# Rows of a rank block in 120 neighbouring partitions instead of two halves of 60, and the fetch of the blocks in four transfers instead of eight

## The chip, the core and the metric

The kernel runs on one core of one Trainium2 chip. Time is device time in microseconds (us), from the first to the last thing that the program does on that core. Several runs are timed and their median is given; one more execution is recorded by the hardware profiler, and all views of the profile come from that execution.

## The reference

For each of 32 batches x is a matrix of 512 channels by 1024 nodes, and adj is 512 by 512. Two layers follow each other, each with a residual sum and a layer norm over the 1024 nodes:

```python
# layer 0
q = einsum('c,bcn->bn', wq, x)
k = einsum('c,bcn->bn', wk, x)
scores = leaky_relu(q[:, None, :] + k[:, :, None], 0.01)   # m by n
att = softmax(scores, axis=-1)
agg = einsum('bcn,bmn->bcm', x, att)
x = layernorm(x + relu(einsum('oc,bcm->bom', adj, agg) + bm[None, :, None]))
# layer 1
x = layernorm(x + (einsum('bnf,nm->bmf', x, adj * adj) + bias))
```

The score of a pair (m, n) is q[n] + k[m]. Where the sum is positive its exponential is exp(q[n]) times exp(k[m]); where it is negative it is exp(0.01 q[n]) times exp(0.01 k[m]). So if the nodes n are sorted by q, what node m needs is one sum over the nodes with the largest q, weighted by exp(q), and one over the rest, weighted by exp(0.01 q). The kernel never forms the 1024 by 1024 attention matrix: it makes tables of these running sums, and each node m picks its rows from them.

## The kernel before

All numbers of lines are those of the profile.

**Tiles and stages of one batch.** `project` (L329) multiplies x by the transposed adj and by wq and wk on TensorE (PE). `keep` brings the result into `zrow`: 1024 rows of 514 numbers, q, then 512 projected values, then a 1. `place` (VectorE, L394) counts for every node its rank by q. `send` (GpSimd, L406) scatters the rows of `zrow` by rank into a buffer `td` in DRAM; `td` has for every rank three rows side by side: the row itself and two places for table rows. `fetch` (L445 to L460) brings the rows back in the order of rank into `zs`. `weigh_exp` (L467, ScalarE) makes the weights `w`, `weigh_by` (L479, L487, VectorE) makes from them and the triangular masks `tri` the small matrices `lw` that sum within a block. `table` (L501, PE) multiplies, `table_out` (L513, ScalarE) copies the product out of PSUM, `carry` (L519) puts the running total into the next block, `table_store` (L527, SyncE's queue, SP) writes table rows to `td`. `pick` (L534, GpSimd) gathers for every node m its own row and two table rows, `scale` and `gain` (L573, L578) mix them, `turn` (L587) transposes, `add` (L594) adds x. The second layer is `multiply` (L666) and the two layer norms are around it.

**Blocks.** The 1024 ranks are cut into nine blocks of R = 120 (the last holds 64). A block is one column of `zs`: its ranks lie in the partitions, in two halves of RH = 60. Half 0 lies in partitions 1 to 60, half 1 in 65 to 124. Partition 0 holds the running total that the sum from the top (i = 0) brings from the block above, partition 64 that of the sum from the bottom (i = 1). The rest are fillers of weight zero. One table row is made for every second rank, so a block gives 60 rows of each table.

**Steps.** `blocks(step)` names the two blocks of a step: 8 - step for the sum from the top and step for the sum from the bottom. `t0` to `t8` are the nine steps of `table`; both products of a step go to one PSUM tile, rows 0 to 63 and 64 to 127. `e0` to `e8` are `table_out`. After each step but the last, `cp` (carry i = 0, on GpSimd) copies row 0 of the result into partition 0 of block 7 - step, and `ca` (carry i = 1, on ScalarE) copies row 64 into partition 64 of block step + 1. At step 3 both go to block 4. The next step waits for its two carries.

**The fetch.** `fetch` issues eight transfers on SP: the last block in two pieces (60 rows and 4), then blocks 0 and 1, block 7, and blocks 2 to 6, each of these once for half 0 and once for half 1. Part 0 of the weights (`wx0`, `wb0`) needs all but blocks 2 to 6, and `t0` needs `wb0`. Part 1 (`wx1`, `wb1`) needs blocks 2 to 6 and is needed at `t2`.

**The order of the work** is written out by hand: the strings BEGIN, SLOT and END list the steps, and each engine runs its instructions in that order. SLOT is the steady state. It works on four batches at once: in one pass the ranks of batch s + 2 are made and sent, the tables of s + 1 and the second layer of s are made, and the output of s - 1 is stored. `fe` (fetch) is SLOT's last step; `wx0 wb0 t0` of the same batch come early in the next pass. Around step 3 the plan reads:

```python
    # SLOT: ... t3 k1u2 k1p5 gb5 p24 gb4 e3 ca3 u0 ts3 cp3 av2 so3 t4 ad0 ...
    # END:  ... @31 e2 ca2 cp2 t3 e3 ca3 cp3 @29 av0 ro1 @31 t4 ...
```

Waits between engines follow from what overlaps: a copy that writes a partition which another copy has written before it in this order waits for that one. SP has eight semaphores for its transfers in turn, so a transfer also waits until the eighth before it has landed.

Of the kernel before, what the change touches and what calls it, by code (L numbers as in the profile page):

```python
# [13 lines left out]
ALU = mybir.AluOpType  # L14
# [9 lines left out]
def gat_gcn_resnorm_kernel(  # L24
# [11 lines left out]
    nc = tc.nc  # L36
    P = 128
    B, C, N = x.shape
# [5 lines left out]
    ZW = C + 2  # L44
    ZB = ZW + 1
    SC = 32.0
    G = P // 2
    RH = 60
    R = 2 * RH
    NB = N // R + 1  # L50
    LAST = N - (NB - 1) * R
# [23 lines left out]
    for i, a in enumerate((wq, wk, bm)):  # L75
        nc.scalar.dma_start(
            out=vec[i * CT : (i + 1) * CT, :], in_=a.rearrange("(t p) -> t p", p=P)
# [6 lines left out]

    tri = const.tile([P, 2, G], F32, name="tri")
    nc.vector.memset(tri, 1.0)
    for half in range(2):
        p0 = half * G
        nc.gpsimd.affine_select(
            out=tri[p0 : p0 + G, 0, :], in_=tri[p0 : p0 + G, 0, :], pattern=[[-2, G]],  # L90
            compare_op=ALU.is_ge, fill=0.0, base=half * RH, channel_multiplier=1,
        )
        nc.gpsimd.affine_select(
            out=tri[p0 : p0 + G, 1, :], in_=tri[p0 : p0 + G, 1, :], pattern=[[2, G]],
            compare_op=ALU.is_ge, fill=0.0, base=-2 - half * RH, channel_multiplier=-1,
        )
    nc.vector.memset(tri[:, :, 0:1], 1.0)
    for row, i in ((0, 0), (G, 1)):
        nc.vector.memset(tri[row : row + 1, i, :], 1.0)
        nc.vector.memset(tri[row : row + 1, 1 - i, :], 0.0)  # L100

    el = const.tile([P, 2], F32, name="el")
    nc.vector.memset(el[:, 0:1], 1.0)
    nc.vector.memset(el[:, 1:2], NEG_SLOPE)
    nc.vector.memset(el[0:1, :], 0.0)
    nc.vector.memset(el[G : G + 1, :], 0.0)
    nel = const.tile([P, 2], F32, name="nel")
    nc.vector.tensor_scalar(nel, el, -1.0, None, ALU.mult)

# [3 lines left out]
        out=first, in_=first, pattern=[[-1, 2 * N - P]], compare_op=ALU.is_ge,  # L113
        fill=0.0, base=N - P - 1, channel_multiplier=1,
# [3 lines left out]
    zs = const.tile([P, NB, ZB], F32, name="zs")  # L118
    nc.vector.memset(zs, 0.0)
    nc.vector.memset(zs[:, :, 0:1], FAR)  # L120
    nc.vector.memset(zs[:, :, C + 1 : ZW], 1.0)
    for row in (0, G):
        nc.vector.memset(zs[row : row + 1, :, C + 1 : ZW], 0.0)

    xs, vs = {}, {}
    for b in range(B):
# [15 lines left out]
    for td in tdb:  # L142
        nc.sync.dma_start(
            out=td.rearrange("(s u) c -> s u c", u=3)[N:NS, 0, :], in_=zs[P + N - NS : P, 0, 0:ZW]
        )
        odd = td.rearrange("(s w u) c -> s w (u c)", w=2, u=3)
        for r in range(0, NS // 2, P):
            n = min(P, NS // 2 - r)
            nc.sync.dma_start(
                out=odd[r : r + n, 0, ZW : 3 * ZW].rearrange("p (j c) -> p j c", j=2)[:, :, 0:1],  # L150
                in_=zs[0:n, 0:2, 1:2],
            )
            nc.sync.dma_start(
                out=odd[r : r + n, 1, ZW : 3 * ZW].rearrange("p (j c) -> p j c", j=2),
                in_=zs[0:n, 0:2, 0:ZW],
# [289 lines left out]
    def fetch(b):  # L445

        zd = tdb[b % 2].rearrange("(s u) c -> s u c", u=3)
        full = zd[0 : (NB - 1) * R, 0, :].rearrange("(j q p) c -> q p j c", q=2, p=RH)
        for half in range(2):
            r = (NB - 1) * R + half * RH  # L450
            n = min(RH, N - r)
            nc.sync.dma_start(
                out=zs[half * G + 1 : half * G + 1 + n, NB - 1, 0:ZW], in_=zd[r : r + n, 0, :]
            )
        for j0, j1 in ((0, 2), (NB - 2, NB - 1), (2, NB - 2)):
            for half in range(2):
                nc.sync.dma_start(
                    out=zs[half * G + 1 : half * G + 1 + RH, j0:j1, 0:ZW],
                    in_=full[half, :, j0:j1, :],
                )  # L460

    some_blocks = (((NB - 2, NB), (0, 2)), ((0, NB - 2), (2, NB)))

# [27 lines left out]
    def blocks(step):  # L491
        return NB - 1 - step, step
# [22 lines left out]
    def carry(b, step, i, by):  # L515

        ts, row, to = tss[b, step], i * G, blocks(step)[i] - 1 + 2 * i
        copy = by.copy if by is nc.scalar else by.tensor_copy
        copy(zs[row : row + 1, to, 1:ZW], ts[row : row + 1, 0 : ZW - 1])  # L519

    def table_store(b, step):

        ts = tss[b, step]
        td = tdb[b % 2].rearrange("(s w u) c -> s w u c", w=2, u=3)
        for i, j in enumerate(blocks(step)):
            n = RH if j < NB - 1 else TL
            nc.sync.dma_start(  # L527
                out=td[j * RH : j * RH + n, 0, 1 + i, 1:ZW],
                in_=ts[i * G + 1 : i * G + 1 + n, 0 : ZW - 1],
            )  # L530

    def pick(b, mt):
# [229 lines left out]
    for name, f in (  # L762
        ("pk", peak), ("qb", spread), ("mx", widen), ("mr", highest), ("ql", line), ("en", ends),
        ("fe", fetch),
    ):
        also(2, name, f)
# [16 lines left out]
    for k in range(NB):  # L783
        also(1, f"t{k}", table, k)
        also(1, f"e{k}", table_out, k)
        if k < NB - 1:
            also(1, f"cp{k}", carry, k, 0, nc.gpsimd)
            also(1, f"ca{k}", carry, k, 1, nc.scalar)
        also(1, f"ts{k}", table_store, k)
# [70 lines left out]
    pi3 @2 p23 @0 pi7 @2 p17 @0 pi5 @2 k1u2 p16 @1 c4 @0 pi6 @1 t1 @2 k1p5 @1 wx1 @0 pi4 @2 p24 @1  # L860
    wb1 c5 @2 p20 p12 p25 p21 p13 @0 oa0 ox0 sx no0 @2 k122 @0 sc0 @2 k112 @1 e1 @2 p27 @0 ga0 sc2
    @1 ts1 ca1 cp1 @0 sc1 gb0 @1 t2 @0 ga1 gb1 @1 e2 @0 sc3 @2 k111 @1 cp2 ca2 @0 ga2 @1 t3 @0 ga3
    gb3 @2 p26 @0 oa1 @1 e3 @0 ox1 @1 cp3 @0 no1 gb2 sc4 sc5 ga4 sc6 ga5 @1 ca3 @0 ga6 sc7 @1 t4 @0
    gb5 @1 c6 @0 ga7 gb4 gb7 @1 e4 @0 gb6 u0 @1 ca4 ts4 @2 k121 @1 cp4 ts3 c7 @0 ad0 @1 t5 ts2 @0 u1
    @1 sh e5 @0 sq0 u2 @1 cp5 @0 ad1 @1 ca5 t6 @0 rt0 @3 ld0 @2 en @0 ad2 sq1 @2 pk @0 u3 @1 e6 @3
    ld1 @2 mx @1 ca6 cp6 @0 sB @2 mr @0 sq2 rt1 ad3 @1 t7 @0 qw5 @3 ld2 @1 e7 @0 sA @1 ts6 @0 rt2 y0
# [99 lines left out]
```

## Time and profile before

| | us |
|---|---|
| median of three runs | 2206.71 (2205.52 to 2206.83) |
| the profiled execution | 2203.48 |
| its span | 2201.8 |
| PE busy | 2109.1 (96%) |
| VectorE (DVE) busy | 1776.1 (81%) |
| ScalarE (ACT) busy | 1653.9 (75%) |
| GpSimd (POOL) busy | 986.5 (45%) |

Busy means that an instruction of the engine runs; weight loads (PEld) are listed apart and lie beside the matmuls. A line of the timeline gives start and duration in us, engine, line, operation, what it writes and reads, the shape, and in brackets how long the engine stood idle before it and what ended that. A line of the waits gives who waited for whom, us in total, times, and the longest. A line of the DMA issues gives how many, the size of one, and the median us from issue to landing. In "DMA packets" the bytes moved and the mean rate of a stretch are given, and under it each queue's packets, MB and share of the time of the 16 DMA engines: q1 is SP's, q0 GpSimd's.

### The profile page before, as it was taken

How to read it: one execution, taken by the hardware profiler on the slowest of the kernel's cores; microseconds unless marked ns; L12 is line 12 of the kernel's file. 1: busy time of each engine (PE TensorE's matmuls, PEld its weight loads, DVE VectorE, ACT ScalarE, POOL GpSimd, SP SyncE). 2: the span in 40 equal slices, each digit the busy share in tenths (PEclk: the TensorE clock that was granted, in tenths of full speed). 3: DMA queues.
4: the chain of work that ended last, by engine and by line, in shares of the span. 5: the costliest groups of instructions: out<-in, count | busy, mean ns of one | idle time of the engine just before them, and what ended most of it. 6: DMA issues, size and time to landing. Idle time of an engine off the chain costs nothing.

```text
span 2201.8 us, 35460 instructions
## 1 busy us (share of the span) xinstructions
PE 2109.1 (96%) x11697; PEld 1235.6 (56%) x11697; DVE 1776.1 (81%) x3576; ACT 1653.9 (75%) x2758; POOL 986.5 (45%) x1291
## 2 busy tenths in 40 slices
PE   7879999999999999999999999999999999999877
PEld 5446555566555566555566555556555556655433
DVE  7568888888888888888888888788888888888666
ACT  1577777887777887777887777888777788777765
POOL 1344455443455444445443445444445544445442
PEclk9989999999999999999999999999999999999998
DMA  7568888777888778888877889878888877888762
GB/s 249 162 224 255 263 272 280 260 236 244 263 257 280 251 240 256 262 260 280 259 244 239 270 255 282 264 244 245 263 256 279 278 247 238 260 264 270 220 206 96
DMA packets 178768, 548.84 MB, mean 249 GB/s; under 512 B 27020, under 2 KB 27032, under 8 KB 178584
## 3 DMA queue, kind: packets, MB, share of 16 engines
q1 hardware_dynamic: 121216, 277.05, 43.8%
q0 software_dynamic: 57344, 269.52, 34.4%
q8 instruction: 93, 1.52, 0.3%
q14 instruction: 91, 0.75, 0.1%
q10 hardware_dynamic: 24, 0.01, 0.0%
HBM read 338.17 MB, written 208.30 MB: 248 GB/s over the span
## 4 chain that ended last, share of the span: by engine, by line
PE 73%; ACT 8%; DMA 5%; issue 4%; DVE 4%; POOL 4%; SPq 1%; POOLq 0%; DVEq 0%; ACTq 0%
PE zp_A L329 17%; PE oA L666 15%; PE tp L501 12%; PE zp_B L329 7%; PE oB L666 7%; PE op L587 5%; PE zp_C L329 4%; PE oC L666 4%; DMA zs<-td 3%; ACT rows L573 1%; ACT y L619 1%; DMA td<-zrow,ranki 1%; ACT v L689 1%; POOL zs L519 1%; PE qb L367 1%
## 5 line engine op out<-in xcount | busy, mean ns | idle before, releaser
L578 DVE SCALAR_TENSOR_TENSOR rows<-rows,ra 128x512 f32<-128x512 f32 x512 | 365.7, 738 | 19.5 <-ACT rows L573 15.7
L501 PE MATMUL tp<-zs,lq 128*64 128x257 f32 x2304 | 338.3, 394 | 27.3 <-POOL zs L519 16.6
L406 POOL DMA_INDIRECT td<-zrow,ranki x256 | 268.3, 1048 | 213.7 <-DVE idx L430 80.2
L666 PE MATMUL oA<-y,adj_sb 128*128 128x512 f32 x768 | 352.2, 601 | 9.8 <-ACT y L619 5.9
L534 POOL DMA_INDIRECT rows<-td,idx x256 | 297.2, 1161 | 90.2 <-issue 68.7
L394 DVE SCALAR_TENSOR_TENSOR junk<-qb,zrow,first 128x1024 int8<-128x1024 f32 x240 | 307.0, 1279 | 10.9 <-PE qb L367 4.0
L519 POOL COPY zs<-ts 1x513 f32<-1x513 f32 x128 | 92.0, 719 | 477.9 <-ACT ts L513 477.7
L329 PE MATMUL zp_A<-wb,x 128*64 128x257 f32 (+1 forms) x1536 | 280.3, 388 | 13.9 <-ACT v L689 6.5
L419 ACT ACTIVATE junk<-lq,kc 128x1024 int8<-128x1024 f32 x240 | 274.5, 1144 | 2.0
L594 DVE SCALAR_TENSOR_TENSOR y<-op,nbm,x 128x1024 f32<-128x1024 f32 x128 | 163.8, 1282 | 128.8 <-PE op L587 128.6
L666 PEld LDWEIGHTS oA<-y,adj_sb 128*128 128x128 f32 x768 | 146.5, 192 | 189.0 <-issue 139.5
L501 PEld LDWEIGHTS tp<-zs,lq 128*64 128x64 f32 x2304 | 171.1, 137 | 135.1 <-POOL zs L519 37.0
L573 ACT ACTIVATE rows<-rows,ra 128x512 f32<-128x512 f32 x256 | 180.0, 718 | 80.0 <-DVE ra L566 78.4
L329 PEld LDWEIGHTS zp_A<-wb,x 128*64 128x64 f32 (+1 forms) x1536 | 178.6, 155 | 77.4 <-ACT v L689 17.8
L350 ACT COPY zrow<-zp_A 128x514 f32<-128x514 f32 x192 | 112.7, 587 | 143.6 <-PE zp_A L329 129.8
L519 POOL COPY zs<-zs 1x513 f32<-1x513 f32 x128 | 79.0, 617 | 253.3 <-ACT zs L513 253.3
L619 ACT ACTIVATE y<-y,nb,r 128x1024 f32<-128x1024 f32 x128 | 158.8, 1241 | 4.3
L695 DVE BATCH_NORM_STATS2 st<-v 128x6 f32<-128x512 f32 x240 | 151.8, 674 | 0.0
L603 ACT ACTIVATE x<-y,nm 128x1024 f32<-128x1024 f32 x128 | 147.2, 1150 | 4.2
L719 ACT ACTIVATE v<-v,nb,rs 128x1024 f32<-128x1024 f32 x120 | 148.1, 1234 | 2.3 <-DVE nb L711 1.4
L587 PE MATMUL op<-ident,rows 128*128 128x128 f32 x1024 | 141.5, 283 | 4.2 <-DVE rows L578 2.0
L587 PEld LDWEIGHTS op<-ident,rows 128*128 128x128 f32 x1024 | 114.9, 143 | 46.0 <-issue 24.6
(162 smaller groups left out, 3802.6 us busy)
## 6 DMA issues: line engine op xcount, KB each, us to landing
x<-in_x_dram SPq DMA_DIRECT2D x128, 512.0 KB, 4.5
out_dram<-v SPq DMA_DIRECT2D x120, 512.0 KB, 2.9
zs<-td SPq DMA_DIRECT2D x64, 602.3 KB, 9.5
td<-zs SPq DMA_DIRECT2D x288, 120.2 KB, 4.3
td<-ts SPq DMA_DIRECT2D x224, 120.2 KB, 2.0
zs<-td SPq DMA_DIRECT2D x64, 240.9 KB, 6.9
zs<-td SPq DMA_DIRECT2D x96, 120.5 KB, 7.2
td<-zs SPq DMA_DIRECT2D x8, 514.0 KB, 7.6
```

The costliest lines, as they stand in the source:

```text
L329: nc.tensor.matmul(zp[n : n + wide, m, 0:CE], side(b, g, a)[:, c, m * P + n : m * P + n + wide], wb[:, w, c, :], start=first and c == 0, s ...
L394: nc.vector.scalar_tensor_tensor(junk(b)[:, 0:N], qbs[b], zrow[:, nt, 0:1], first[:, o : o + N], ALU.subtract, ALU.is_lt, accum_out=rank[: ...
L406: sc = nc.gpsimd.indirect_dma_start(out=td[:, :], out_offset=bass.IndirectOffsetOnAxis(ap=ranki[:, nt : nt + 1], axis=0), in_=zrow[:, nt, ...
L419: nc.scalar.activation(junk(b)[:, N : 2 * N], qs[b], AF.Sign, bias=kcs[b][:, nt : nt + 1], accum_out=signs(b)[:, nt : nt + 1],)
L501: nc.tensor.matmul(tp[i * G : (i + 1) * G, h, 0:CE], lw[:, ks[i], :], zs[:, j, 1 + h * CE : 1 + (h + 1) * CE], start=True, stop=True,)
L519: copy(zs[row : row + 1, to, 1:ZW], ts[row : row + 1, 0 : ZW - 1])
L534: nc.gpsimd.indirect_dma_start(out=rows[:, mt, :], out_offset=None, in_=tdb[b % 2].rearrange("(s u) c -> s (u c)", u=3), in_offset=bass.In ...
L573: nc.scalar.activation(u, u, AF.Copy, scale=ratios(b)[:, k, 1:2])
L578: nc.vector.scalar_tensor_tensor(u, rg[:, k, i, 1 : C + 1], ratios(b)[:, k, i : i + 1], u, ALU.mult, ALU.add)
L587: nc.tensor.transpose(op[:, mt * P : (mt + 1) * P], rg[:, mt, 1, 1 + ot * P : 1 + (ot + 1) * P], ident)
L619: nc.scalar.activation(yall[:, ot], yall[:, ot], AF.Identity, bias=nb, scale=r)
L666: nc.tensor.matmul(o[:, m, :], quarters[w][:, a, m * P : (m + 1) * P], part(b, y)[:, a, :], start=fresh and a == 0, stop=a == CT // 2 - 1, ...
```

## The change

The ranks of a block now lie in partitions 2 to 121, one behind the other. Both running totals lie in front of them, in partitions 0 (from the top) and 1 (from the bottom). The masks `tri`, the scales `el` and the zeroed last column follow this layout. In the sum from the bottom the total is now made in row 1 of its half of the product (row 65 of the tile), and row 64 is zero. `carry` for i = 1 copies both rows into partitions 0 and 1 of the next block: it writes a zero into partition 0 as well. The table rows of that half begin one partition later, and `table_store` reads them there. `fetch` takes the last block in one transfer of 64 rows and the other blocks in three transfers of 120 partitions. In BEGIN the step `ca3` of batch 1 moves forward, ahead of `cp3`; in SLOT and END the order is as before.

```diff
-    for half in range(2):
-        p0 = half * G
-        nc.gpsimd.affine_select(
-            out=tri[p0 : p0 + G, 0, :], in_=tri[p0 : p0 + G, 0, :], pattern=[[-2, G]],
-            compare_op=ALU.is_ge, fill=0.0, base=half * RH, channel_multiplier=1,
-        )
...
-    nc.vector.memset(tri[:, :, 0:1], 1.0)
-    for row, i in ((0, 0), (G, 1)):
-        nc.vector.memset(tri[row : row + 1, i, :], 1.0)
-        nc.vector.memset(tri[row : row + 1, 1 - i, :], 0.0)
+    nc.gpsimd.affine_select(
+        out=tri[:, 0, :], in_=tri[:, 0, :], pattern=[[-2, G]],
+        compare_op=ALU.is_ge, fill=0.0, base=-1, channel_multiplier=1,
+    )
...
+    for i in range(2):
+        nc.vector.memset(tri[:, i, i : i + 1], 1.0)
+        nc.vector.memset(tri[0:2, i, i:], float(i))
+        nc.vector.memset(tri[0:1, i, :], 1.0 - i)
...
-    nc.vector.memset(el[0:1, :], 0.0)
-    nc.vector.memset(el[G : G + 1, :], 0.0)
+    nc.vector.memset(el[0:2, :], 0.0)
...
-    for row in (0, G):
-        nc.vector.memset(zs[row : row + 1, :, C + 1 : ZW], 0.0)
+    nc.vector.memset(zs[0:2, :, C + 1 : ZW], 0.0)
...
         zd = tdb[b % 2].rearrange("(s u) c -> s u c", u=3)
-        full = zd[0 : (NB - 1) * R, 0, :].rearrange("(j q p) c -> q p j c", q=2, p=RH)
-        for half in range(2):
-            r = (NB - 1) * R + half * RH
-            n = min(RH, N - r)
-            nc.sync.dma_start(
-                out=zs[half * G + 1 : half * G + 1 + n, NB - 1, 0:ZW], in_=zd[r : r + n, 0, :]
-            )
+        full = zd[0 : (NB - 1) * R, 0, :].rearrange("(j p) c -> p j c", p=R)
+        nc.sync.dma_start(out=zs[2 : 2 + LAST, NB - 1, 0:ZW], in_=zd[(NB - 1) * R : N, 0, :])
         for j0, j1 in ((0, 2), (NB - 2, NB - 1), (2, NB - 2)):
-            for half in range(2):
-                nc.sync.dma_start(
-                    out=zs[half * G + 1 : half * G + 1 + RH, j0:j1, 0:ZW],
-                    in_=full[half, :, j0:j1, :],
-                )
+            nc.sync.dma_start(out=zs[2 : 2 + R, j0:j1, 0:ZW], in_=full[:, j0:j1, :])
...
-        copy(zs[row : row + 1, to, 1:ZW], ts[row : row + 1, 0 : ZW - 1])
+        copy(zs[0 : 1 + i, to, 1:ZW], ts[row : row + 1 + i, 0 : ZW - 1])
...
-                in_=ts[i * G + 1 : i * G + 1 + n, 0 : ZW - 1],
+                in_=ts[i * G + 1 + i : i * G + 1 + i + n, 0 : ZW - 1],
...
-    gb3 @2 p26 @0 oa1 @1 e3 @0 ox1 @1 cp3 @0 no1 gb2 sc4 sc5 ga4 sc6 ga5 @1 ca3 @0 ga6 sc7 @1 t4 @0
+    gb3 @2 p26 @0 oa1 @1 e3 @0 ox1 @1 ca3 cp3 @0 no1 gb2 sc4 sc5 ga4 sc6 ga5 ga6 sc7 @1 t4 @0
```

## The prediction

> **What bounds the kernel now.** First the page: the busy times, then the chain that ended last.
>
> ```profile
> span 2201.8 us, 35460 instructions
> PE 2109.1 (96%) x11697; PEld 1235.6 (56%) x11697; DVE 1776.1 (81%) x3576; ACT 1653.9 (75%) x2758; POOL 986.5 (45%) x1291
> PE 73%; ACT 8%; DMA 5%; issue 4%; DVE 4%; POOL 4%; SPq 1%; POOLq 0%; DVEq 0%; ACTq 0%
> ```
>
> TensorE (PE) is busy 96% of the span and in the steady batches almost without a hole: a first table product to the next batch's first takes 65.0 us at best. So an edit counts only by the time that it makes PE wait, or spares it. The view of waits shows the two places that this change touches:
>
> ```profile
> POOL zs L519 <- ACT ts L513: 477.7, 125, 15.0
> PEld tp L501 <- POOL zs L519: 37.0, 57, 2.9
> PE tp L501 <- POOL zs L519: 16.6, 23, 2.4
> ACT w L467 <- DMA zs<-td: 16.2, 11, 6.4
> ```
>
> (total us, times, longest.) GpSimd's carry copies (POOL, L519) have no slack to give: PE already waits for some of them. The fetch (DMA zs<-td) is late for the weights `w` in only 11 batches of 32.
>
> **The new wait: `cp3` behind `ca3`.** Of each batch's eight pairs of carries seven write different blocks. At step 3 both write block 4. Before, one wrote partition 0 and the other 64, side by side. After, ScalarE's copy writes partitions 0 and 1 (partition 0 with a zero), so GpSimd's copy into partition 0 must come behind it, and `t4` needs both. The timeline of one steady batch around step 3:
>
> ```profile
> 1059.21 0.61 ACT L513 COPY ts<-tp 128x514 f32<-128x514 f32 x1
> 1059.86 0.62 ACT L519 COPY zs<-ts 1x513 f32<-1x513 f32 x1
> 1059.88 0.71 POOL L519 COPY zs<-ts 1x513 f32<-1x513 f32 x1 [2.00 <-ACT ts L513]
> 1059.91 1.09 PE L587 MATMUL op<-ident,rows 128*128 128x128 f32 x8
> 1060.94 1.09 PE L501 MATMUL tp<-zs,lq 128*64 128x257 f32 x8
> 1061.05 1.28 DVE L594 SCALAR_TENSOR_TENSOR y<-op,nbm,x 128x1024 f32<-128x1024 f32 x1 [0.92 <-PE op L587]
> ```
>
> (start, duration in us.) `e3`, then both carries together, then `t4` at 1060.94 with no wait: PE had come from `u0` (L587). After: the ACT copy ends at 1060.48. GpSimd starts 0.06 later (what it now takes from the end of `e3`). Its copy takes 0.605, its duration at steps 4 and 5, where no VectorE instruction lies beside it. PE starts 0.054 after its end, the shortest distance in the trace. 1060.48 + 0.06 + 0.605 + 0.054 = 1061.20, against 1060.94: PE waits 0.26 us. The same sum with medians over the steady batches (ACT copy's end to `t4` now 0.465, after 0.720) gives 0.255. PE runs in order and everything behind `t4` hangs on it, `e4` and both carries of step 4 included, so I count it in full: 28 batches (2 to 29) x 0.255 = 7.1; batch 30 has 0.506 now, so 0.2; batch 31, where `t4` starts 0.10 after the ACT copy, 0.6 (and GpSimd's `ro1` behind the copy as much later). Batch 0: GpSimd is late there anyway (0.725 after `e3`), nothing. Sum **+8.0 us**.
>
> Here a rule is weighed. Where VectorE reads two SBUF tensors, GpSimd's copy is longer:
>
> ```profile
> 1115.68 0.69 DVE L318 TENSOR_TENSOR rows<-rows,x 128x512 f32<-128x512 f32 x1
> 1115.80 1.03 POOL L519 COPY zs<-ts 1x513 f32<-1x513 f32 x1 [7.86 <-ACT ts L513]
> ```
>
> The Trainium skill (SBUF — State Buffer, "SBUF: two separate sides") says why: the two engines share one pair of SBUF ports, locked for a whole instruction, for VectorE operations with two SBUF inputs. At its new place `cp3` meets only L594, 0.51 us in, which reads PSUM and one SBUF tensor. By the rule the copy stays at 0.605; with the row's 1.03 the wait would be 0.68 and the sum +20. I take 0.605: L594 starts later than the copy.
>
> **The fetch.** Eight transfers become four: 64, 120x2, 120 and 120x5 rows instead of 60 + 4, twice 60x2, twice 60, twice 60x5. The bytes are the same.
>
> ```profile
> zs<-td SPq DMA_DIRECT2D x64, 602.3 KB, 9.5
> zs<-td SPq DMA_DIRECT2D x64, 240.9 KB, 6.9
> zs<-td SPq DMA_DIRECT2D x96, 120.5 KB, 7.2
> ```
>
> SP issues: 8 x some 0.4 to 0.7 us before, half after. SP then idles until the first `ts` store 9 to 14 us later, so this is worth nothing; the stores behind have fewer earlier transfers to wait for, and nobody waits for them (`e2` shows no DMA wait). What can count is the landing. By the semaphore updates in the trace the six transfers that `wx0` needs have landed, at the median of batches 3 to 27, 6.8, 5.3, 7.6, 8.8, 9.6 and 10.3 us after the first issue, the last two (for `wx1`, `t2`) at 13.4 and 15.6. `t2` starts at 18: those are covered. `wx0` starts at about 10.3, so the sixth is just in time, and where it is late PE waits:
>
> ```profile
> 1179.04 0.67 ACT L467 ACTIVATE w<-zs,bw,el 128x2 f32<-128x2 f32 x2 [1.29 <-DMA zs<-td]
> 1179.46 0.57 DVE L479 TENSOR_TENSOR lq<-tri,w 128x128 f32<-128x128 f32 x2 [1.21 <-ACT w L467]
> 1179.81 1.14 PE L501 MATMUL tp<-zs,lq 128*64 128x257 f32 x7 [0.79 <-DVE lq L479]
> ```
>
> These holes before `t0` are 0.29, 1.72, 0.37, 0.79, 0.20 and 0.74 us (batches 6, 7, 14, 17, 27, 31): 4.1 us is all that a faster fetch can give in the steady part and the end. How much faster? Moved by the DMA queues in 1171.5 to 1178, the fetch alone, and in 1060 to 1065, stores and loads of 128 partitions with a few table stores:
>
> ```profile
> DMA packets 663, 1.24 MB, mean 190 GB/s; under 512 B 70, under 2 KB 70, under 8 KB 663
> q1 hardware_dynamic: 657, 1.21, 98.9%
> ...
> DMA packets 519, 1.63 MB, mean 325 GB/s; under 512 B 62, under 2 KB 62, under 8 KB 519
> q1 hardware_dynamic: 519, 1.63, 85.2%
> ```
>
> The engines are full both times, yet the fetch moves half as much: 190 against 325/0.85 = 382 GB/s. The second rule: the Trainium skill (SBUF — State Buffer, "Door 1: The DMA port swizzle") says that a transfer into partitions 0 to 63 or 64 to 127 reaches 8 of 16 ports, at most 218 GB/s, all 128 reach 436. By the rule, 120 partitions go at up to the 382 of the row; the 740 KB between first and sixth landing (3.5 us, 211 GB/s) take 1.9 us, 1.6 less. By a row of this kernel nothing is shown: no transfer of it has 120 partitions, and rows dealt out in runs may crowd one port as now. Bounds: 0 and 1.6 us; I take 0.8, the middle, as neither end has a nearer row. That returns 0.29 + 0.8 + 0.37 + 0.79 + 0.20 + 0.74 = **-3.2** (0 to -4.0).
>
> At the start, batch 0's `wx1` waits 1.78 us on ACT for the last transfer (1.23 MB in 6.6 us), and VectorE's `lq` and ranks queue behind it; batch 1's `wx0` waits 6.41 us and GpSimd's carry and gathers stand behind. Both lie on the chain. Bounds 0 and -3.0; I take **-1.3**, since other waits lie close by.
>
> **At nothing.** Two selects and a memset fewer: all setup runs in the first 10 us, under the load of x that PE waits for until 11.6 (cover gone: 0.07 us a memset). Two partitions in ScalarE's copy: 128x514 takes 0.59, 1x513 0.62, so partitions are free. Table stores start one partition later, same bytes. The order of POOL, PE and SP is kept; in BEGIN `ca3` of batch 1 goes ahead of three scalings (ACT L573). `t4` of batch 1 waits 2.7 us for it now, but the chain there runs through those scalings and VectorE's gains (L578), and ACT has 1.5 us free before the first of them, so 0.62 fits: 0, at best -1.
>
> **Sum.** 2203.48 (the profiled execution, span 2201.8) + 8.0 - 3.2 - 1.3 = 2207.0, that is +3.5. The median of the runs is 2206.71, 3.2 above the profiled one; the same +3.5 on it gives **2210.2 us** (+0.16%). About 0.2% (4.4 us) is what a measurement of this kernel can tell from no change.
>
> **Rivals.**
> - *The fetch is no faster* (15 to 16 full engines crowd the same ports or memory as before). For: engines at 98.9% now; against: the 382 of the other window. Then only some 0.5 comes back: +7.5, 2214.2. Chance 0.25.
> - *Faster: the wait at `t4` is absorbed.* Later in the batch PE sometimes waits for ScalarE's `y` (oC, 0.4 to 1.7 us in six batches, near 6 us in all), and a later `t4` would only shorten that. Against: those `y` stand behind `e4` and its successors, which move with `t4`. If it held, below 0.16 us a batch the fetch's 4.5 decide; at 0 it is 2202.2. Chance 0.11.
> - *GpSimd's copy is held at its new place* by VectorE (1.03 us, row above): +20 - 4.5, 2222. Against: in the timeline of step 3 L594 starts behind it. Chance 0.08.
> - *Main case*, +1.5 to +6 (2208.2 to 2212.7): chance 0.50, a third of it above 4.4. Rest 0.06, both ways.
>
> Slower by over 0.2%: 0.17 + 0.25 + 0.08 + 0.02 = 0.52; faster: 0.08 + 0.02 = 0.10; within: 0.38. The range 2202.5 to 2219 leaves out the held copy and the strongest absorption.
>
> **What would show it.** Right: at step 3 the POOL copy starts 0.06 after the end of ScalarE's, `t4` has a hole of some 0.25 us ended by POOL zs, PE's wait for POOL zs grows by 7 to 8 us; the sixth landing's counterpart (the third transfer) comes 0.4 to 1.6 us earlier and the holes before `t0` are nearly gone. Wrong: a POOL copy of 1 us there, no hole at `t4`, holes before `t0` as large as now, or holes where there were none.

## The result and the profile after

The changed kernel takes 2213.09 us (median of 8 runs, 2210.9 to 2217.0); the kernel before 2201.98 (8 runs). The ratio is 1.0052, 95% interval 1.0035 to 1.0068: 0.5% slower, some 11 us. Measured a second time (`c_again`, below) it is 1.0042 [1.0027, 1.0057]. The forecast was 2210.2 us (+3.5), with a range of 2202.5 to 2219 and "slower" as the likeliest side. The time lies in the range, nearest to the rival "the fetch is no faster" (2214.2); as a difference, +11 is more than the forecast's +3.5 and the rival's +7.5.

The profiled execution took 2213.49 us, its span 10.0 us more than before. The page first:

```profile
span 2211.8 us, 35261 instructions
...
PE 2113.3 (96%) x11665; PEld 1246.2 (56%) x11697; DVE 1778.6 (80%) x3575; ACT 1652.4 (75%) x2758; POOL 983.2 (44%) x1289
...
PE 68%; ACT 8%; DMA 8%; issue 5%; DVE 5%; POOL 5%; SPq 1%; POOLq 0%; ACTq 0%; DVEq 0%
```

PE is still the bound; its share of the chain that ended last fell from 73% to 68%, those of DMA and POOL rose. The view of waits says who made PE wait (us in total, times, longest):

```profile
POOL zs L506 <- ACT zs L506: 83.9, 31, 3.9
...
PEld tp L488 <- POOL zs L506: 48.3, 87, 2.5
...
PE tp L488 <- POOL zs L506: 21.7, 49, 2.0
...
ACT w L454 <- DMA zs<-td: 16.4, 17, 6.4
```

(L506 is `carry`, L488 `table`, L454 `weigh_exp`.) The first line is new: GpSimd's carry waits for ScalarE's carry, once in all batches but one. PE's waits for that copy rose from 16.6 us in 23 places to 21.7 in 49. The last line was meant to shrink and did not: 16.2 us in 11 places before, 16.4 in 17 after. Step 3 of the same steady batch as before, in the timeline:

```profile
1059.94 0.61 ACT L500 COPY ts<-tp 128x514 f32<-128x514 f32 x1
...
1060.58 0.62 ACT L506 COPY zs<-ts 2x513 f32<-2x513 f32 x1
...
1061.26 0.60 POOL L506 COPY zs<-ts 1x513 f32<-1x513 f32 x1 [2.65 <-ACT zs L506]
...
1061.77 1.28 DVE L581 SCALAR_TENSOR_TENSOR y<-op,nbm,x 128x1024 f32<-128x1024 f32 x1 [0.92 <-PE op L574]
...
1061.92 1.09 PE L488 MATMUL tp<-zs,lq 128*64 128x257 f32 x8 [0.18 <-POOL zs L506]
```

The two carries lie one behind the other, and `t4` stands 0.18 us until GpSimd's ends. By medians over the steady batches `t4` now starts 0.719 us after the end of ScalarE's copy (before 0.465; forecast 0.720), GpSimd's copy lasts 0.604 (forecast 0.605), and the shortest time from one batch's first product to the next's is 65.26 us against 65.00. That is more than the 0.18 of the hole because PE's matmuls overlap: from the start of the matmul ahead of `t4` to that of `t4` it is 0.457 us, in the kernel before 0.203.

The fetch, a late one in the timeline and then its issues on the page:

```profile
523.88 0.67 ACT L454 ACTIVATE w<-zs,bw,el 128x2 f32<-128x2 f32 x2 [1.71 <-DMA zs<-td]
524.30 0.57 DVE L466 TENSOR_TENSOR lq<-tri,w 128x128 f32<-128x128 f32 x2 [1.62 <-ACT w L454]
...
524.65 1.14 PE L488 MATMUL tp<-zs,lq 128*64 128x257 f32 x7 [1.20 <-DVE lq L466]
```

```profile
zs<-td SPq DMA_DIRECT2D x32, 1204.7 KB, 13.8
...
zs<-td SPq DMA_DIRECT2D x32, 481.9 KB, 8.1
zs<-td SPq DMA_DIRECT2D x32, 240.9 KB, 8.7
```

By the semaphore updates the first three transfers, all that `wx0` needs, have landed 10.30 us after the first issue (median of batches 3 to 27); before, the sixth of eight landed at 10.28. The last lands at 14.6 instead of 15.6, where it was covered anyway. The holes before `t0` add up to 5.5 us (batches 2 to 31), before 4.1.

So the wait came as worked out, and what was to pay for half of it did not. Two questions for experiments: is the wait the whole loss, and why is a fetch in blocks of 120 no quicker?

### The profile page after: what moved, and what is told of

Its sections match the earlier page's. It is cut to its first block, busy times and chain, and to the rows that moved or that the text cites. A ratio compares the mean times of both kernels' runs of the same rounds, so it can differ in the third digit from the quotient of the medians.

```text
span 2211.8 us, 35261 instructions
## 1 busy us (share of the span) xinstructions
PE 2113.3 (96%) x11665; PEld 1246.2 (56%) x11697; DVE 1778.6 (80%) x3575; ACT 1652.4 (75%) x2758; POOL 983.2 (44%) x1289
## 4 chain that ended last, share of the span: by engine, by line
PE 68%; ACT 8%; DMA 8%; issue 5%; DVE 5%; POOL 5%; SPq 1%; POOLq 0%; ACTq 0%; DVEq 0%
PE zp_A L325 15%; PE oA L653 14%; PE tp L488 12%; PE zp_B L325 7%; PE oB L653 6%; PE op L574 4%; PE zp_C L325 4%; DMA zs<-td 4%; PE oC L653 3%; DMA td<-zrow,ranki 2%; POOL zs L506 2%; ACT y L606 1%; POOL rows L521 1%; DVE junk L390 1%; ACT v L676 1%
## 5 line engine op out<-in xcount | busy, mean ns | idle before, releaser
L488 PE MATMUL tp<-zs,lq 128*64 128x257 f32 x2304 | 342.6, 396 | 30.2 <-POOL zs L506 21.7
L506 POOL COPY zs<-ts 1x513 f32<-1x513 f32 x128 | 87.4, 683 | 502.7 <-ACT ts L500 418.8
L488 PEld LDWEIGHTS tp<-zs,lq 128*64 128x64 f32 x2304 | 174.3, 138 | 139.6 <-POOL zs L506 48.3
L506 POOL COPY zs<-zs 1x513 f32<-1x513 f32 x128 | 78.6, 614 | 244.7 <-ACT zs L500 244.7
## 6 DMA issues: line engine op xcount, KB each, us to landing
zs<-td SPq DMA_DIRECT2D x32, 1204.7 KB, 13.8
```

The lines of the kernel that those rows point to most:

```text
L488: nc.tensor.matmul(tp[i * G : (i + 1) * G, h, 0:CE], lw[:, ks[i], :], zs[:, j, 1 + h * CE : 1 + (h + 1) * CE], start=True, stop=True,)
L506: copy(zs[0 : 1 + i, to, 1:ZW], ts[row : row + 1 + i, 0 : ZW - 1])
```

## Experiments

All ratios are to the kernel before, run beside each kernel on the same chip.

**The wait alone, in the layout before (`e2_wait`).** One edit in `carry`:

```diff
+        if step == 3 and b != 1:
+            if i == 1:
+                thirds[b] = made
+            else:
+                tc.add_manual_dep(
+                    made.ins, thirds.pop(b).ins.name,
+                    mybir.DependencyInfo(mybir.DependencyClass.Sync, mybir.DependencyReason.DATA),
...
```

> The kernel before, with nothing but the wait added: at step 3 GpSimd's carry copy waits until ScalarE's is done (all batches but batch 1, where the order would have to change). Theory of the wait: the hole of 0.18 us before t4 appears, a batch takes 65.27 instead of 65.0 us, and the kernel is 7.5 to 8.5 us slower than before. Rival (the fetch or the rows' place makes the difference): at most 2 us slower.

Measured: 1.0041 [1.0025, 1.0057]. The timeline of its step 3 is that of the changed kernel:

```profile
1064.58 0.62 ACT L520 COPY zs<-ts 1x513 f32<-1x513 f32 x1
...
1065.26 0.60 POOL L520 COPY zs<-ts 1x513 f32<-1x513 f32 x1 [2.65 <-ACT zs L520]
...
1065.91 1.09 PE L502 MATMUL tp<-zs,lq 128*64 128x257 f32 x8 [0.18 <-POOL zs L520]
```

Least period 65.26 us, sixth landing 10.22. The wait alone gives the slowdown of the whole change within the intervals. What the fetch and the start are worth the ratios do not settle here, since each interval is some 3.5 us wide to either side; `f_cover3` (below) settles it better.

**Eight transfers in the new layout (`e3_eight`).** `fetch` cut at 60 rows again (the last block likewise, not shown):

```diff
-            nc.sync.dma_start(out=zs[2 : 2 + R, j0:j1, 0:ZW], in_=full[:, j0:j1, :])
+            for r in (0, RH):
+                nc.sync.dma_start(
+                    out=zs[2 + r : 2 + r + RH, j0:j1, 0:ZW], in_=full[r : r + RH, j0:j1, :]
+                )
```

> The changed kernel with the fetch cut again into eight transfers (60 and 4 rows, then twice 60 rows for each group of blocks), into partitions 2 to 61 and 62 to 121. If four transfers instead of eight bring nothing, as the landings say (third of four at 10.30 us after the first issue, sixth of eight at 10.28), the time is that of the changed kernel within 2 us (+9 to +13 us against the kernel before). If larger transfers land sooner and gave something back, this one is slower than the changed kernel by 2 to 4 us. If transfers of 120 partitions are themselves a cost, it is faster by 2 to 4 us.

Measured: 1.0090 [1.0072, 1.0109], slower than any of the three theories had it; that larger transfers land sooner came nearest. The sixth transfer lands at 10.55 and the last at 15.9, holes before `t0` 5.7 us. In this layout four transfers are some 8 us better than eight; against eight in the layout before they bring nothing. By the two profiles it is 6.8 us, and 5.4 of these lie in one batch, 13, which takes 71.92 us (66.52 in the changed kernel):

```profile
986.49 0.17 DVE L543 TENSOR_TENSOR s<-rows,kc 128x4 f32<-128x4 f32 x1 [3.71 <-DMA rows<-td,idx]
...
987.74 2.71 PE L325 MATMUL zp_A<-wb,x 128*64 128x257 f32 x9 [3.15 <-DVE zrow L344]
```

With the fetch in flight (from 977.8) the gathers came late, VectorE (DVE) waited for them and made `zrow` late, PE stood for 3.15 us, and from 987.4 on its granted clock was 0.50 for 3.4 us. Whether this comes in every execution, and why the same pieces do worse at partitions 2 to 61 and 62 to 121 than at 1 to 60 and 65 to 124, no run shows.

**Transfers alone (`e4_transfers`).** A kernel that only fetches, five blocks at a time, and computes nothing of the reference.

> No layer is computed: only transfers from DRAM, five blocks each, one after the other with nothing beside them, four times over. Forms: two of 60 partitions (1 to 60, 65 to 124); 120 partitions from partition 2; 120 from 0; 128; 112; then 120 from 2 and 128 with the rows close together in DRAM instead of 6168 bytes apart; the same two with rows of 2048 instead of 2056 bytes; 60 alone. 1.23 MB in 120 partitions. If the partitions reached set the rate: two of 60 some 6 us or more from issue to landing, 128 some 4.5, and 120 between them; the forms of the rows in DRAM make no difference. If the rows in DRAM set the rate, 120 and 128 from the spread rows take as long per byte as two of 60, and the close or the even rows are faster.

The issues on its page (how many, KB each, median us to landing):

```profile
zs<-td SPq DMA_DIRECT2D x8, 1204.7 KB, 8.2
zs<-td SPq DMA_DIRECT2D x12, 602.3 KB, 5.4
zs<-td SPq DMA_DIRECT2D x4, 1285.0 KB, 5.9
zs<-dense SPq DMA_DIRECT2D x4, 1285.0 KB, 6.2
zs<-even SPq DMA_DIRECT2D x4, 1280.0 KB, 6.0
zs<-dense SPq DMA_DIRECT2D x4, 1204.7 KB, 8.2
zs<-even SPq DMA_DIRECT2D x4, 1200.0 KB, 8.2
zs<-td SPq DMA_DIRECT2D x4, 1124.4 KB, 6.4
```

Where the rows lie in DRAM (thirds of wider rows, dense, rows of 2048 bytes) changes nothing, nor does the first partition (the eight of 1204.7 KB began at 0 and at 2). The number of partitions does: 128 take 5.9 us, 112 take 6.4, and 120, with fewer bytes than 128, 8.2, not between 128 and two of 60 as expected but above both. Of two of 60 issued together the second lands at 7.9 (the 5.4 is the median over all transfers of 60). That is the result in small: one transfer of 120 is as slow as the pair of 60 that it replaced. The sixteen increments of a transfer's semaphore hint at a cause: for 120 and for 60 partitions one comes 0.5 us after the issue and fifteen at the end; for 128 and 112 all sixteen come at the end. The Trainium skill (DMA: Bandwidth & Descriptors, "Why a DMA increments its semaphore by 16 and not by 1") says that such a transfer is shared among k DMA engines, the largest number up to 16 that divides its slowest dimension, and that the rest of the sixteen counts at once: 15 for 120 and for 60, 16 for 128 and 112. The counts agree. But 8 rows a block on each of 15 engines should then take as long as 8 on each of 16, 5.9 us. The view of windows for one transfer of 120 and one of 128 (window, us, busy VectorE and GpSimd, granted clock, share of the 16 DMA engines' time, GB/s):

```profile
108.10:116.10 8.00, 0.06 (x1) 0.00 (x0) 1.00 0.73 154
125.00:130.90 5.90, 0.06 (x1) 0.00 (x0) 1.00 0.67 223
```

For 600 rows the engines were busy 0.73 x 16 x 8.0 = 93 us, 0.156 us a row; for 640 rows 63 us, 0.099 a row. Each row takes half as long again. The same skill page ("The descriptor swizzle") says that a transfer of 128 partitions is dealt out so that each engine writes to one SBUF port of its own; that could be such a difference, which no view here shows directly.

**More shapes (`d_shapes`)**, to tell the number of engines from how rows are dealt out; it computes nothing of the reference either.

> Transfers alone again, nothing else is computed: five blocks a transfer, 2056-byte rows of the table (one third of each rank, as the kernel fetches them), one transfer at a time, four times each: 128 partitions, 120 from partition 2, 112 from 0 and from 2, 104, 96, 80, 64, 60, and two of 64 at once. Before: 128 took 5.9 us, 112 took 6.4, 120 took 8.2, 60 took 5.2. Theory that the number of engines decides (rows an engine: 128 over 16 is 8, 120 over 15 is 8): 104 rows over 13 engines, 8 rows each, would take 5.9, and 120 would have too, which it did not. Theory that an engine's time grows with its rows unless the transfer has 128 partitions, which are dealt out by ports: 104 takes about 8, 96 (6 rows each) about 5.5 to 6, 80 (5 rows) about 5, 64 (4 rows) 4.2 or as 60, and only 128 is out of line; where 112 begins makes no difference. Theory that only those counts that give all sixteen engines work are quick: 96, 80 and 64 in proportion to 112 (5.5, 4.6, 3.7), 104 slow like 120. Two of 64 at once: 5.9 if each keeps to its own half of the engines' ports, 7 to 8 if they are in each other's way as two of 60 were (7.9).

```profile
zs<-td SPq DMA_DIRECT2D x8, 1124.4 KB, 6.2
zs<-td SPq DMA_DIRECT2D x12, 642.5 KB, 7.0
zs<-td SPq DMA_DIRECT2D x4, 1285.0 KB, 5.9
zs<-td SPq DMA_DIRECT2D x4, 1204.7 KB, 8.2
zs<-td SPq DMA_DIRECT2D x4, 1044.1 KB
zs<-td SPq DMA_DIRECT2D x4, 963.8 KB, 6.2
zs<-td SPq DMA_DIRECT2D x4, 803.1 KB, 5.7
zs<-td SPq DMA_DIRECT2D x4, 602.3 KB, 5.1
```

104 partitions (1044.1 KB, no landing on the page) landed after 8.1 us by the updates, like 120: the number of engines alone is out, since 13 engines with 8 rows each should have taken 5.9. The two theories that remain are half right: 112, 96, 80 and 64 all take 5.7 to 6.2, nowhere near in proportion to rows. 64 alone take 5.7, so half the partitions bring half the bytes in the time of all 128. That agrees with the port rule weighed in the prediction, if the fullest ports set the time: from 64 partitions on, the eight ports of partitions 0 to 63 have all their rows. The rule does not give the two of 64 at once, which lie in different halves and take 8.3 (the 7.0 is the median over both), nor 120 and 104. Those two are the counts with 8 rows a block on each of 15 or 13 engines, and 2.2 to 2.3 us slower than 128; the other counts below 128 have 7 or fewer. Engines that crowd the same ports, as the prediction's rival has it, would fit; no run shows which port an engine writes.

**The fetch in 128 partitions (`c_wide`)**, with the changed kernel again (`c_again`) beside it. Partition p of block j takes rank 120 j + p - 2; partitions 0 and 1 are overwritten by the carries, 122 to 127 get weight nought, and the table in DRAM has two ranks of padding ahead (not shown).

```diff
+    nc.gpsimd.affine_select(
+        out=tri, in_=tri, pattern=[[0, 2], [0, G]],
+        compare_op=ALU.is_ge, fill=0.0, base=R + 1, channel_multiplier=-1,
+    )
...
-            nc.sync.dma_start(out=zs[2 : 2 + R, j0:j1, 0:ZW], in_=full[:, j0:j1, :])
+            nc.sync.dma_start(out=zs[0:P, j0:j1, 0:ZW], in_=full(j0, j1))
```

> The changed kernel once more, as it was measured, on the chip of the three runs beside it. Every theory expects what its first measurement gave: 1.0035 to 1.0068 of the kernel before, some 11 us more, a hole of about 0.18 us on TensorE ahead of t4 in each steady batch, the third transfer of the fetch landing 10.3 us after the first was issued, and holes before t0 that add up to some 3 to 4 us. It is the base from which the other three runs are read.

> The changed kernel with the three transfers of whole blocks widened from 120 to 128 partitions: partition p of block j takes rank 120 j + p - 2, so partitions 0 and 1 (carried rows, overwritten before they are used) and 122 to 127 (weight nought by one more affine_select at the start) take neighbouring ranks too, and the table in DRAM has two ranks of padding ahead. Rows, gathers and scatters are the same otherwise. In the transfers measured alone, 120 partitions landed after 8.2 us with one of the sixteen semaphore increments at 0.5 us, and 128 partitions after 5.9 us with all sixteen at the end. Theory that the shape is why the prediction's earlier landing failed: the third transfer lands 1.5 to 2.3 us earlier than 10.3, the last about 3 us earlier than 14.6, the holes before t0 (3 to 4 us in all) go, and the kernel is 2 to 4 us faster than the changed kernel, the wait at t4 remaining (1.003 to 1.004). Rival, that the fetch waits for something ahead of it in the DMA engines (the gathers and the table's stores): landings within 0.5 us of the old ones, time as the changed kernel. Rival, that it lands earlier and the holes move elsewhere: earlier landings, same time.

`c_again`: 1.0042 [1.0027, 1.0057]. `c_wide`: 0.9997 [0.9987, 1.0007], by the medians 7.8 us less than `c_again` (2200.61 and 2208.39). The third transfer lands at 7.64 us (`c_again` 9.56), the last at 11.2 (14.4), though more bytes are moved. The waits of `c_wide`:

```profile
PEld tp L507 <- POOL zs L525: 55.4, 93, 2.7
...
PE tp L507 <- POOL zs L525: 23.0, 54, 2.0
...
ACT w L473 <- DMA zs<-td: 5.0, 1, 5.0
```

Of the 10 to 17 late fetches one is left, in batch 1; the hole at `t4` is untouched. The gain is twice the forecast of 2 to 4 us. Batch 0 takes 37.4 us from its first product to the next batch's (`c_again` 39.9, before 40.8). And what the 25 steady periods have above the shortest one sums to 4.6 us, against 13.9 before and 12.4 and 6.2 in the two profiles of the changed kernel, so a late fetch also cost time in places that are not the hole before `t0`. VectorE's wait for the gathers (`rows<-td,idx`) can be a part of it: from 200 to 2020 us it is 4.6 us in the changed kernel, 3.7 in `c_again`, 2.2 in `c_wide`. The rest stays open.

**Covers for the hole at `t4`.** Three kernels move a part of a projection ahead of `t4`, in SLOT only: `e1_cover` one column half of p20, `c_cover2` the first half of p20's contraction, `f_cover3` that of p21 (shown).

```diff
-    ca3 u0 ts3 cp3 av2 so3 t4 ad0 so2 p21 so0 e4 ts2 ca4 u1 cp4 sq0 t5 ad1 p20 ld0
+    ca3 u0 ts3 cp3 av2 so3 p21a t4 ad0 so2 p21b so0 e4 ts2 ca4 u1 cp4 sq0 t5 ad1 p20 ld0
```

> The changed kernel, with half of the projection p20 (four matmuls of 64 columns, some 0.43 us of PE work) moved in SLOT from between t5 and t6 to just ahead of t4, so that PE has work while GpSimd's carry copy runs behind ScalarE's. Nothing else differs. Theory of the wait (the carry copy behind the other one is the cost): the hole of 0.18 us before t4 is gone in 28 batches, the product-to-product time of a batch goes from 65.27 back to 65.0 us, and the kernel is 7 us faster than the changed one, so +3 to +5 us against the kernel before (whose eight runs have a median 11.1 us below the changed kernel). Rival (the new fetch is the cost, the wait only moves idle time about): no gain, +9 to +13 us against the kernel before.

> The changed kernel with the narrow projection p20 cut in two by the contraction instead of by columns: its first two matmuls (first half of the contraction, both column halves side by side) go ahead of t4, its other two stay behind u1. Only the order of TensorE changes, in 28 batches. Theory that the wait of cp3 is the whole loss: the hole before t4 is gone, the least time from product to product falls from 65.27 to about 65.0 us, and the kernel is 7 us faster than the changed kernel, within some 2 to 4 us of the kernel before (1.001 to 1.002). Rival, that the cover itself costs TensorE time as the cut by columns did: t4 has no hole, but the period stays at 65.2 or more and the time at 1.005. Rival, that the loss is not at t4: the hole goes and the time stays.

> The changed kernel with another cover at t4: of the wide projection p21, which follows t4, the first half of the contraction (0.48 us of TensorE) goes ahead of t4 and the other half stays. t5 had 0.46 us between the end of its carry and its start, so it loses at most a few hundredths; t6, which the cover before this one made late, is left alone. Theory that the wait of cp3 is what the steady batches lost: no hole at t4, least period back at 65.0 to 65.05 us instead of 65.27, and the time some 6 us under the changed kernel (1.001 to 1.003), unless the transfers' landings use the time up, which the periods above the least one would show (6 to 14 us over 25 batches so far). Rival, that a steady batch needs 65.2 us anyway: period as with the cover before, time 1.004.

All three fill the hole, and only the last is worth it. `e1_cover`: 1.0116 [1.0095, 1.0137]; least period 65.87, so PE had 0.6 us more to do in each batch: the two column halves of a narrow projection run side by side (in the changed kernel's trace their matmuls start in pairs within 0.01 us, one pair every 0.21 us), and cut apart they do not. `c_cover2`: 1.0038 [1.0028, 1.0048]; least period 65.15 and a new wait at `t6`, which now comes too soon after its carry:

```profile
1066.08 0.60 POOL L506 COPY zs<-zs 1x513 f32<-1x513 f32 x1 [2.36 <-ACT zs L500]
1066.74 0.63 PEld L488 LDWEIGHTS tp<-zs,lq 128*64 128x64 f32 x8 [0.18 <-POOL zs L506]
```

By the period it should still have gained some 3 us; the interval of the ratio does not exclude that. `f_cover3`: 1.0011 [0.9999, 1.0023], least period 65.01. With the hole at `t4` filled the changed kernel is level with the kernel before, to 0.2%: the wait was the loss, now shown from both sides. The interval (-0.2 to +5.1 us) leaves no room for the 4.5 us that fetch and start were to give back. The same cover in the kernel before was not run; its period of 65.00 us leaves no hole there to fill. Landings (10.2 us) and the waits for the fetch (15 times, 15.2 us) stay as they were.

**Both at once.** `c_both` is `c_wide` with the cover of `c_cover2`, `f_both3` with that of `f_cover3`.

> Both edits of the two runs before in one kernel: 128 partitions in the fetch, and two matmuls of p20 ahead of t4. If both theories hold the gains add: 7 us from the hole at t4 and 2 to 4 us from the landings, so that the kernel is level with the kernel before or up to 2 us under it (0.999 to 1.001). If only the cover works, 1.001 to 1.002; if only the fetch, 1.003 to 1.004; if neither, 1.005.

> This cover and the fetch of 128 partitions in one kernel. The fetch alone gave 0.9997 of the kernel before with a least period of 65.26 us and 4.6 us over it in 25 batches; with the period at 65.0 to 65.05 the time is 5 to 6 us less: 0.997 to 0.998 of the kernel before, about 2195 us. Rival, that the cover gives only what the one before gave with the wide fetch: 0.999.

`c_both`: 0.9993 [0.9982, 1.0004]. `f_both3`: **0.9963 [0.9948, 0.9978]**, 2193.36 us against 2202.65, better than both kernels. Its step 3 in the timeline, and its fetch issues:

```profile
1050.53 0.62 ACT L525 COPY zs<-ts 2x513 f32<-2x513 f32 x1
...
1051.21 0.61 POOL L525 COPY zs<-ts 1x513 f32<-1x513 f32 x1 [2.67 <-ACT zs L525]
...
1051.52 0.60 PE L334 MATMUL zp_B<-wb,rows 128*128 128x257 f32 x2
...
1052.05 1.09 PE L507 MATMUL tp<-zs,lq 128*64 128x257 f32 x8
```

```profile
zs<-td SPq DMA_DIRECT2D x32, 1285.0 KB, 9.5
...
zs<-td SPq DMA_DIRECT2D x32, 514.0 KB, 6.0
zs<-td SPq DMA_DIRECT2D x32, 257.0 KB, 6.2
```

The carries still lie one behind the other, but PE has p21's first half to do meanwhile. The transfers take 9.5, 6.0 and 6.2 us instead of 13.8, 8.1 and 8.7.

**The fetch in halves of 64, in the layout before (`d_before_wide`).**

```diff
...
+        rows64(0, 0, 2)
+        nc.sync.dma_start(out=zs[G + 1 : G + 1 + RH, 0, 0:ZW], in_=zd[2 + RH : 2 + R, 0, :])
+        rows64(0, NB - 2, 1)
+        rows64(1, 1, 2, NB - 3)
+        for half in range(2):
+            rows64(half, 2, NB - 4)
```

> The kernel before, its layout and the order of its table kept (so no wait of cp3 behind ca3), with its six transfers of 60 partitions for whole blocks changed to five of 64 and one of 60 (block 0's second half, whose carried row has to start at nought), the ranks beside each half weighted with nought, two ranks of padding in the table in DRAM. Eight transfers as before. If the shape of the fetch is worth the same without the new wait: the sixth transfer lands some 2 us before 10.3, the holes before t0 (4 us) and part of what follows them go, the least period stays at 65.0 us, and the kernel is 5 to 9 us faster than the kernel before (0.996 to 0.998). If 64 partitions are no quicker than 60, because only 128 are dealt out well: landings as before, 1.000.

Measured: 1.0042 [1.0025, 1.0058]. The sixth transfer lands at 10.8, later than 10.3, and the holes before `t0` grow to 7.6 us. Neither theory had it slower. `d_shapes` agrees with the later landing: one transfer of 64 takes 5.7 us where 60 take 5.1, and two at once 8.3 where two of 60 took 7.9. In the profile, batch 14 (69.73 us, before 65.26) has the chain of events of `e3_eight` again: gathers late, PE standing for 2.71 us, then 3.4 us at half clock. The table's padding, the same as in `c_wide`, is not what gained there, and sixteen engines are not enough; it was the 128 partitions in one transfer.

## Why the prediction was right or wrong

- **The number: in the range, with some luck.** The forecast added 3.5 us to 2206.71, the median of three runs of the kernel before; that of all eight is 2201.98. The change is +11.1 us (7.7 to 15.0 by the interval), against +3.5, so the absolute time looks closer than the forecast was.
- **The wait at `t4`, +8.0 us: right.** Place, length and reason came as written: GpSimd's copy starts 0.06 us after the end of ScalarE's, takes 0.604, PE loses 0.25 a batch (forecast 0.255). Only the view of waits grew less than forecast, by 5.1 us instead of 7 to 8, since it counts the 0.18 of the hole. The wait alone measured 1.0041, some 9 us.
- **The weighed rule on the shared SBUF ports: agrees.** GpSimd's copy at its new place met no VectorE instruction with two SBUF inputs and kept its 0.60. The rival of the held copy (2222) is out.
- **The rival "the wait is absorbed": did not come.** Each steady batch kept its 0.26 us.
- **The fetch 0.8 us earlier, -3.2 us: the step that failed.** The third transfer landed at 10.30 us (in a later profile of the changed kernel 9.56, and with the covers 9.89 to 10.18), the sixth before at 10.28 (10.22 in `e2_wait`); 0.8 us earlier it came in none. The holes before `t0` were to be nearly gone and were 3.5 to 5.5 us in these five profiles, 4.1 and 4.2 in those of the old fetch. I had set the end at 0 because "no transfer of it has 120 partitions", and the other at 1.6 from a rate of 382 GB/s that stores and loads of 128 partitions reached; the middle was a guess between them. Alone, 120 partitions move at 154 GB/s and 128 at 223. The rate of 128 partitions could not be carried over to 120; what slows 120 down stays open (above).
- **All that a faster fetch can give is 4.1 us in the steady part and the end: too small.** `f_cover3` and `f_both3` differ in the fetch alone, and from batch 2's first product to batch 30's they take 1833.5 and 1824.6 us: 8.9 us, of which 2.9 are holes before `t0`. Beside it, batch 0 takes 2.5 us less in `c_wide` than in `c_again`.
- **The start, -1.3 us: came and went.** From batch 0's first product to batch 1's it is 0.7 us less; batch 1, up to its successor's first product, has 1.4 more (86.7 against 85.3).
- **The end.** In batch 31 `t4` is 0.6 us later, as forecast. The whole stretch from its first product on is 3.0 us longer; 2.1 of this lies between `t1` and `t2`, where the clock was halved (below).
- **At nothing.** ScalarE's copy of two partitions takes 0.62 us like that of one; setup and table stores show nowhere.

The 10 us between the two spans are 0.8 up to batch 2's first product, 6.5 from there to batch 30's and 2.7 behind it: the wait's 8 or somewhat less, about 0 instead of -4.5 for fetch and start, and some 2 us of clock in this profile.

## What to carry to other kernels

Fewer transfers alone brought nothing here; their shape did: look in your own trace for a transfer with exactly the number of partitions that you mean to use, or measure one alone, before you count on its rate; here it paid to fetch 8 useless rows a block to get from 120 partitions to 128. Where two copies must follow each other into one place, the engine that waits for the second needs other work of just that length: taking half a contraction of p21 was free, while half the columns of p20 cost more than the hole, and half its contraction, owed to a later step that has no slack, brought next to nothing (1.0038 against 1.0042).

## What was not expected of the hardware

PE's granted clock falls to half for stretches of 3.4 to 13.7 us at the start and the end of each profile of the whole kernels, and twice in the middle (`e3_eight`, `d_before_wide`, above), where PE has holes. One such stretch lies across batch 31's `t1` in the changed kernel; the kernel before has full clock there (first the changed kernel, then the one before; window, us, busy us of PE, PEld, DVE, ACT and POOL, granted clock, DMA share, GB/s):

```profile
2100.00:2107.00 7.00, 6.05 (x16) 2.29 (x18) 5.05 (x11) 3.06 (x7) 4.43 (x6) 0.52 0.73 215
```

```profile
2093.00:2098.00 5.00, 3.62 (x16) 1.55 (x18) 4.31 (x10) 3.65 (x7) 3.66 (x6) 1.00 0.64 160
```

The same sixteen matmuls are in both. In `c_again` and `f_both3` that stretch has full clock, but a halved one of 13.65 us begins 11 to 12 us behind batch 31's first product, and there `t4` to `t5` takes 3.4 us instead of 2.5. The lengths (3.41, 6.83, 10.24, 13.65 us) are multiples of one window, and all 101 stretches in the twelve profiles begin on a grid of 3.413 us. In the window ahead of each, PE was busy for at most 1.67 us, about half of it; only nine windows at full clock with so little (1.48 to 1.65 us) were not followed by one. That agrees with the Trainium skill (TensorE: Matmul & The Clock Gate, "Part 1: The HAM clock gate"), by which PE's activity is judged over free-running windows of some 3.4 us, so where a stretch falls differs from run to run. In batches 2 to 29 of the other ten profiles no hole was longer than 1.73 us and no stretch was halved. Whether the change has a part in the one at batch 31's `t1` stays open.
